# Loading and folding the forward stage's first unit inside the convolution, and squaring into v's far tile

## The chip, the cores and the metric

The kernel runs on one core of one Trainium2 chip. The metric is the device time of one launch in microseconds (us), the median of several runs. Engines are called as in the profile: PE is TensorE (PEld its weight loads), DVE is VectorE, ACT is ScalarE, POOL is GpSimd, SP is SyncE, which here issues most of the DMA transfers; SPq, ACTq and POOLq are the queues of transfers that these engines issue.

## The reference

Two residual layers work on `x`, 16 images of 16 channels of 256 x 256 points in float32. `_gn` is a group norm over 8 groups of two channels.

```python
# layer 0: a circular 3 x 3 convolution, written with Fourier transforms
x = x + _L0_conv_ref(_gn(x), L0_conv_weight)
# layer 1: a Laplace layer
x = x + _L1_conv_ref(_gn(x), ty, tx, weights_pole1, weights_pole2, weights_residue)

# _L1_conv_ref:
alpha = fft2(_gn(x))                                     # per image and channel
A  = 1 / (omega1 - weights_pole1)                        # omega: 2 pi i x frequency
Bm = 1 / (omega2 - weights_pole2)
S  = einsum('ikpq,oikp,xikq->oxik', weights_residue, A, Bm)
output_residue1 = einsum('biox,oxik->bkox', alpha, S)    # mixes channels, per frequency
C  = einsum('biox,oikp->bikpx', alpha, A)
D  = einsum('bikpx,xikq->bikpq', C, Bm)
output_residue2 = einsum('bikpq,ikpq->bkpq', D, weights_residue)
x1 = ifft2(output_residue1).real
E1, E2 = exp(weights_pole1 * ty), exp(weights_pole2 * tx)
F  = einsum('kbpq,bipz->kbiqz', output_residue2, E1)
x2 = einsum('kbiqz,biqx->kizx', F, E2).real              # the transient part
return x1 + x2 / 256 / 256
```

In what follows, v is the result of layer 0, which is the input of layer 1.

## The kernel before

The kernel has four stages, one after the other: the convolution, the forward transform, the mixing of channels, and the inverse transform. Line numbers are those of the kernel before.

**Order and memory.** Each stage opens its own memory pools under a manual schedule: every engine executes its instructions in the order in which the program writes them, and semaphores are set only where two instructions touch the same data. Pools stand as a stack in on-chip memory: a pool that is opened first lies lowest, and a pool that grows moves all that are opened after it. Pools of one stage lie over those of the stage before. In the later stages a tile waits only for the former users of the bytes that it covers (`reuse_waits="tile"`). Where a pool has several buffers, a new tile takes the oldest one and waits for its readers.

**Convolution** (the loop over g, 24 steps for each of 16 images b). A step is 16 small matmuls (L302), which add up in PSUM banks of `ps_conv`; there are six. v is kept as a sum and a difference of the image's two halves, so that each image has four units of a "pair" half, written by the rows r = 0 and 1, and a "far" half, written by r = 2 and 3 three steps later. ScalarE evicts two banks to the tile `pair` when g % 6 is 5 and two to the tile `far` when g % 6 is 2 (L321). Two steps after the far eviction, `mirror` (L267) has DVE add far to pair (L269) and POOL subtract far from pair (L272). ScalarE then squares both results for the statistics (L280): it needs only the sum that `accum_out` gives, and writes the squares themselves to a tile `junk` in a pool of its own. Both squares stand in a list with the step at which they are issued:

```python
squared.append((g + 5, lambda: square(both, 4 + 2 * u, b, bias=shift2[:, b : b + 1])))
squared.append((g + 7, lambda: square(lo, 5 + 2 * u, b)))
```

Four stores to DRAM, one a step (L331, in the list `folded`), take the pair to `vD`. Beside this, SP loads the images for the next steps in 18 parts each (L130, tile `xt`, five buffers); generators compute the statistics of x, the tables of the later stages (`make_coef`, `make_poles`, `make_hat`, `make_c`, mostly on POOL and DVE, with a store of the table `cD` at L643), and the statistics of v for the first 12 images (`v_stats`, L339).

**Forward stage.** It has 64 units (i, b0), channel i and four images from b0 on. For each unit `load_v` (L740) loads 1 MB of `vD` by two transfers to a tile `s` (pool `fold_y`, three buffers, units loaded up to three ahead). `fold` (L746) folds it on DVE (four instructions at L752, L755, L762, L763, L766) and POOL (L762 and L763 for the other half) through a tile `vf` to a tile `vq` (pool `fold_2`, two buffers). `lines` (L770) multiplies for four images j and two halves xo by a table on PE (L774 and L782, into three banks `ps_y`), and ScalarE evicts each bank to the tile `t`, scaled by v's norm (L790). `columns` (L797) does the same for the unit before along the other axis, with the table `fold2` on PE (L817), and DVE writes the spectrum of channel i to the tile `spec` (32 KB a partition, even channels in the pool `spec_even`, odd ones in `spec_odd`, with a pad of 4 KB between). When a channel is complete, `spec` is stored to `aD`; SP issues this store, for the last channel ScalarE does (L973).

The stage begins with the loads of units 0, 1 and 2 (the first on POOL's queue) and the fold of unit 0:

```python
loaded = {u: load_v(*units[u], nc.sync if u else nc.gpsimd) for u in range(3)}
vq = fold(*units[0], loaded.pop(0))
```

In the loop over units the fold of the unit after the next is written ahead of the lines of the present one. In the first two units `rest` is interleaved with the lines: these are v's statistics for the last four images (DVE L349 to L354, PE L357, DVE L359 to L366, PE L374, then a square root).

**Mix stage.** The table `cD` is loaded to the tile `ct` (32 KB a partition, L1005), `first_sums` and `sums` multiply it by weights `w` (PE L1027), DVE and ScalarE spread the result over a tile `sg` (L1047, L1044), spectra of the 16 channels are loaded in groups `abd` (L1102), and PE mixes the channels for each frequency (L1120). The results are stored to `yD`. **The inverse stage** loads them, transforms back along both axes and adds the transients and v.

Of the kernel before, what the change touches and what calls it, by code (L numbers as in the profile page):

```python
# [9 lines left out]
FP = mybir.dt.float32  # L10
AF = mybir.ActivationFunctionType
ALU = mybir.AluOpType
# [4 lines left out]
B = 16  # L17
C = 16
N = 256
P = 128  # L20
# [4 lines left out]
def conv_then_laplace_kernel(ctx: ExitStack, tc: tile.TileContext, a: dict, out: bass.AP):  # L25
# [15 lines left out]
    nc = tc.nc  # L41
    x = a["x"]
# [11 lines left out]
    def const(name, shape, home=cp):  # L54
        t = home.tile(shape, FP, name=name, tag=name)
        later_loads.append((t, a[name]))
        return t
# [10 lines left out]
    vD = []  # L68
    for b in range(B // 4):
        t = dp.tile([P, C, 8 * N + 256], FP, name=f"vD{b}", tag=f"vD{b}")  # L70
# [21 lines left out]
    ptab = ExitStack()  # L92
    tp = ptab.enter_context(tc.tile_pool(name="tables", bufs=1))
    kmask = const("kmask", [P, C], tp)
    fold2 = const("fold2", [P, 2, 64], tp)
    vmr = tp.tile([P, 2, B, C], FP, name="vmr", tag="vmr")


# [12 lines left out]

    p1 = ExitStack()
    wp = p1.enter_context(tc.tile_pool(name="conv_w", bufs=1))
    xp = p1.enter_context(tc.tile_pool(name="xt", bufs=5))
    vp = p1.enter_context(tc.tile_pool(name="v_pair", bufs=3))
    fp = p1.enter_context(tc.tile_pool(name="v_far", bufs=2))
    jp = p1.enter_context(tc.tile_pool(name="junk", bufs=1))
    sp = p1.enter_context(tc.tile_pool(name="stats", bufs=2))  # L120
    sw = p1.enter_context(tc.tile_pool(name="setup", bufs=1))
    pc = p1.enter_context(tc.tile_pool(name="p_conv", bufs=6, space=PSUM))
# [6 lines left out]
    def load_part(t, b, h, i, j):  # L129
        nc.sync.dma_start(  # L130
            out=t[:, i:j].rearrange("p (n r) x -> p n (r x)", r=2),
            in_=x[b][:, 8 * h + i // 2 : 8 * h + j // 2, 0 : 2 * (N + 2)],
        )
# [131 lines left out]
    shift2 = tp.tile([P, B], FP, name="shift2", tag="shift2")  # L265

    def mirror(g, b, u, pair, hi):  # L267
        both, lo = pair[:, :, :, 0], pair[:, :, :, 1]
        nc.vector.scalar_tensor_tensor(  # L269
            both, lo, 1.0, hi, ALU.mult, ALU.add, accum_out=sums[:, b, u : u + 1]  # L270
        )
        nc.gpsimd.tensor_tensor(lo, lo, hi, ALU.subtract)  # L272
        folded.extend((g + 7 + k, b, u, pair, *divmod(k, 2)) for k in range(4))
        squared.append((g + 5, lambda: square(both, 4 + 2 * u, b, bias=shift2[:, b : b + 1])))
        squared.append((g + 7, lambda: square(lo, 5 + 2 * u, b)))

    def square(t, col, b, **by):

        junk = jp.tile([P, 4, N], FP, name="junk", tag="junk")
        nc.scalar.activation(  # L280
            junk,
            t.rearrange("p r j x -> p (r j) x"),
            AF.Square,
            accum_out=sums[:, b, col : col + 1],
            **by,
        )
# [362 lines left out]
    def chain(*gens):  # L649
        for gen in gens:  # L650
            yield from gen

    ready, acc, later, folded, squared, jobs = {}, {}, [], [], [], []
    for j, (_, piece) in enumerate(x_stats(0)):
        if j == 8:
# [26 lines left out]
    early = v_stats(0, B - 4, lambda: pst.tile([P, 512], FP, name="ps_stat", tag="ps_stat"))  # L682
    for g in range(24 * B + 3):
        conv(g)
        past = g - 24 * (B - 4)
        if past in (12, 17, 20, 25, 28, 31):
            next(early, None)
        b, n = divmod(g, 24)
        if b + 2 < B and n % 12 > 2:
            h, k = n // 12, n % 12 - 3  # L690
            if k == 0:
                halves.setdefault(b + 2, []).append(
                    xp.tile([P, 18, N + 2], FP, name="xt", tag="xt")
                )
            load_part(halves[b + 2][h], b + 2, h, PARTS[k], PARTS[k + 1])
        for b, gen in at_step.get(g, ()):
            going.append([b, gen, next(gen)])
        for it in list(going):
            while it[2] is not None and g >= 24 * it[0] - it[2][0]:
                it[2][1]()  # L700
                it[2] = next(it[1], None)
            if it[2] is None:
                going.remove(it)
        run_jobs(g, (psu,) if n in slots and 12 <= past <= 31 else slots.get(n, ()))
        next(tables, None)
# [7 lines left out]
    p1 = ExitStack()  # L713


    def pool(stage, name, bufs=1, **kw):
        return stage.enter_context(tc.tile_pool(name=name, bufs=bufs, reuse_waits="tile", **kw))

    sp = pool(p1, "fold_y", 3)
    f1 = pool(p1, "fold_1")  # L720
    fp = pool(p1, "fold_2", 2)
    lp = pool(p1, "lines", 2)
    a0 = pool(p1, "spec_even")
    kp = pool(p1, "between")
# [3 lines left out]
    bp = pool(p1, "b_const")  # L728
# [6 lines left out]

    kp.tile([P, 1024], FP, name="between", tag="between")
    sgn = bp.tile([P, 2], FP, name="sgn", tag="sgn")
    m, n = cols[:, 16:17], cols[:, 17:18]

    def load_v(i, b0, eng=nc.sync):  # L740
        s = sp.tile([P, 4, 2, N], FP, name="s", tag="s")
        for j in range(0, 4, 2):
            eng.dma_start(out=s[:, j : j + 2], in_=vD[b0 // 4][:, i, j : j + 2])
        return s.rearrange("p b h x -> p h b x")

    def fold(i, b0, s):  # L746


        vf = f1.tile([P, 2, 2, 4, P], FP, name="vf", tag="vf")
        lo, hi = s[:, :, :, 0:P], s[:, :, :, N - 1 : P - 1 : -1]  # L750
        for j in range(4):
            nc.vector.scalar_tensor_tensor(  # L752
                vf[:, 0, 0, j], lo[:, 0, j], vmr[:, 1, b0 + j, i : i + 1], hi[:, 0, j], ALU.add, ALU.add
            )
        nc.vector.tensor_tensor(vf[:, 0, 1], lo[:, 1], hi[:, 1], ALU.add)  # L755


        vq = fp.tile([P, 2, 2, 4, 2, 64], FP, name="vq", tag="vq")

        def again(xo, eng):  # L760
            lo, hi = vf[:, xo, :, :, 0:64], vf[:, xo, :, :, P - 1 : 63 : -1]
            eng.tensor_tensor(vq[:, xo, :, :, 0], lo, hi, ALU.add)  # L762
            eng.tensor_tensor(vq[:, xo, :, :, 1], lo, hi, ALU.subtract)  # L763

        again(0, nc.vector)
        nc.vector.tensor_tensor(vf[:, 1], lo, hi, ALU.subtract)  # L766
        again(1, nc.gpsimd)
        return vq.rearrange("p e o b h x -> p e o b (h x)")

    def lines(i, b0, vf, t, j):  # L770

# [95 lines left out]
    units = [(i, b0) for i in range(C) for b0 in range(0, B, 4)]  # L867
# [64 lines left out]
        )  # L932
        return wt

    loaded = {u: load_v(*units[u], nc.sync if u else nc.gpsimd) for u in range(3)}
    vq = fold(*units[0], loaded.pop(0))
    nc.vector.memset(sgn[:, 0:1], -1.0)
    nc.vector.memset(sgn[:, 1:2], 1.0)
    rest = v_stats(B - 4, B, lambda: pa.tile([P, 512], FP, name="ps_y", tag="ps_y"))
    last, first_weights = None, weights(0)  # L940
    for u in range(len(units) + 1):
        at = units[u] if u < len(units) else None
        if at is not None:
            now = vq
            t = lp.tile([P, 2, 4, 3, P], FP, name="t", tag="t")
            if u + 1 < len(units):
                vq = fold(*units[u + 1], loaded.pop(u + 1))
                if u + 3 < len(units):
                    loaded[u + 3] = load_v(*units[u + 3])
                if u < 2:  # L950
                    next(rest)
            for j in range(2):
                lines(*at, now, t, j)
        if last is not None:
            i, b0 = last[:2]
            if b0 == 0:
                spec = (a0, a1)[i % 2].tile([P, 2, N, B], FP, name="spec", tag="spec")
                psd = pd.tile([P, B, 32], FP, name="psd", tag="psd")
            done = columns(*last, spec, psd)
        if at is not None:  # L960
            for j in range(2, 4):
                lines(*at, now, t, j)
                if u < 2:
                    next(rest, None)
        if u == len(units) - 4:
            first_constants()
        if len(units) - 4 < u < len(units):
            next(first_weights)
        if last is not None:
            first_slots(b0, spec, *done)  # L970
            if b0 == B - 4:
                project(i, psd)
                (nc.sync if i + 1 < C else nc.scalar).dma_start(  # L973
                    out=aD[:, 2 * i : 2 * i + 2], in_=spec.rearrange("p r f b -> p r (f b)")
                )
        last = (*at, t) if at is not None else None
# [11 lines left out]
    tp = pool(p2, "ct")  # L988
# [232 lines left out]
    for g in range(32):  # L1221
# [5 lines left out]
        for n in range(4):  # L1227
# [4 lines left out]
            for m in range(4):  # L1232
                if evict and m < 2:
                    spread(n, (ahead, [z.rearrange("p q n -> p n q") for z in evict]), odds=(m,))
                o, src = mix(4 * n + m, sg, yt)
# [82 lines left out]
    def combine(b0, yk, step=4):  # L1318

        u = up.tile([P, 4, 4, P], FP, name="u", tag="ud")  # L1320
        for j in range(0, 4, step):
            combine_images(yk, slice(b0 + j, b0 + j + step), u[:, j : j + step])
        return u
# [84 lines left out]
    units = [(k, b0) for k in range(C) for b0 in range(0, B, 4)]  # L1408
# [7 lines left out]
    u = combine(0, yk, 1)  # L1416
# [12 lines left out]
    for n, (k, b0) in enumerate(units):  # L1429
# [5 lines left out]
        if b0 % 8 == 0:  # L1435
            both = transient_x(k, b0)
        hs = both[:, b0 % 8 : b0 % 8 + 4]
        begun = [transient(ey_now[:, j], hs[:, j]) if n == 0 else None for j in range(4)]
        if n + 1 < len(units):
# [3 lines left out]
            u = combine(units[n + 1][1], yk)  # L1443
            load_ahead(n + 1)
        r = rp.tile([P, 4, 2, N], FP, name="r", tag="r")
# [172 lines left out]
```

## Time and profile before

| what | value |
|---|---|
| times of three runs | 2611.66, 2622.16, 2623.72 us |
| median | 2622.16 us |
| profiled execution, its own time | 2615.02 us |
| span of its profile | 2613.2 us, 84,265 instructions |
| mean granted PE clock | 0.984 of full |
| busy: PE | 2458.4 us, 94% of the span |
| busy: PEld (beside PE) | 1894.7 us, 73% |
| busy: DVE | 1971.9 us, 75% |
| busy: ACT | 1436.9 us, 55% |
| busy: POOL | 1259.3 us, 48% |
| moved by DMA | 653 MB, 250 GB/s on average |

The profile is of one execution. Its page cuts the span in 40 slices of 65.3 us and gives each engine's busy share in tenths. The row of PE reads `5999999989999999998999999999699999999998`: it starts with 5, is 8 in the 9th and the 19th slice (the convolution's end at 558 us lies in the former, the forward stage's at 1187 us in the latter), and 6 in the 29th, in the inverse stage. Its PE clock row, which is the clock that the throttle granted in tenths, has an 8 in these three slices and 9 elsewhere. In the other views a group of instructions has its line, engine, operation and tiles (written `out<-in`, with partitions x elements), and in brackets the idle time of the engine just before it with what ended that idle time. Most of PE's idle time is in the first slice and at the places just named.

### The profile page before, as it was taken

How to read it: one execution, taken by the hardware profiler on the slowest of the kernel's cores; microseconds unless marked ns; L12 is line 12 of the kernel's file. 1: busy time of each engine (PE TensorE's matmuls, PEld its weight loads, DVE VectorE, ACT ScalarE, POOL GpSimd, SP SyncE). 2: the span in 40 equal slices, each digit the busy share in tenths (PEclk: the TensorE clock that was granted, in tenths of full speed). 3: DMA queues.
4: the chain of work that ended last, by engine and by line, in shares of the span. 5: the costliest groups of instructions: out<-in, count | busy, mean ns of one | idle time of the engine just before them, and what ended most of it. 6: DMA issues, size and time to landing. Idle time of an engine off the chain costs nothing. (4 is left out here: it accounts for less than half of the span.)

```text
span 2613.2 us, 84265 instructions
## 1 busy us (share of the span) xinstructions
PE 2458.4 (94%) x35314; PEld 1894.7 (73%) x35314; DVE 1971.9 (75%) x3772; ACT 1436.9 (55%) x2599; POOL 1259.3 (48%) x1275
## 2 busy tenths in 40 slices
PE   5999999989999999998999999999699999999998
PEld 2454555567777777775888888888588888888887
DVE  7777789748888888887887788787276676667666
ACT  2566666666666666665666666676244444444443
POOL 1333378332333333333656556555555565655553
PEclk9999999989999999998999999999899999999999
DMA  8888888854654654665777787777988888888884
GB/s 273 276 291 286 294 282 302 282 206 167 242 213 191 258 225 192 228 243 175 219 228 227 227 234 229 222 222 225 260 299 286 292 289 283 296 288 294 288 288 173
DMA packets 318010, 653.16 MB, mean 250 GB/s; under 512 B 49174, under 2 KB 163990, under 8 KB 305728
## 3 DMA queue, kind: packets, MB, share of 16 engines
q1 hardware_dynamic: 316464, 640.57, 72.7%
q8 instruction: 278, 4.55, 0.7%
q0 software_dynamic: 896, 3.02, 0.5%
q10 hardware_dynamic: 272, 4.19, 0.4%
q14 instruction: 100, 0.82, 0.1%
HBM read 368.15 MB, written 280.36 MB: 248 GB/s over the span
## 5 line engine op out<-in xcount | busy, mean ns | idle before, releaser
L1330 POOL TENSOR_TENSOR u<-yk 128x512 f32<-128x512 f32 (+1 forms) x268 | 359.4, 1373 | 309.0 <-PE ps_p L1366 243.9
L1120 PE MATMUL ps_mix<-abd,sg 128*64 128x128 f32 x8192 | 471.4, 276 | 34.3 <-DMA yD<-yt 24.0
L1120 PEld LDWEIGHTS ps_mix<-abd,sg 128*64 128x64 f32 x8192 | 452.9, 138 | 64.7 <-issue 54.2
L302 PE MATMUL ps_conv<-xt,wc 32*32 32x512 f32 x12288 | 443.2, 601 | 31.1 <-issue 25.5
L302 PEld LDWEIGHTS ps_conv<-xt,wc 32*32 32x32 f32 x12288 | 251.5, 103 | 209.6 <-issue 127.0
L790 ACT ACTIVATE t<-ps_y,vmr 128x384 f32<-128x384 f32 x512 | 297.0, 580 | 161.8 <-PE ps_y L782 161.8
L1047 DVE STREAM_SHUFFLE sg<-ps_s 128x512 f32<-128x512 f32 (+1 forms) x264 | 328.5, 1319 | 0.0
L774 PE MATMUL ps_y<-tabE,vq 128*128 128x256 f32 x1024 | 313.5, 388 | 11.1 <-DVE vq L763 9.5
L782 PE MATMUL ps_y<-tabO,vq 128*128 128x256 f32 x1024 | 306.3, 381 | 0.0
L1390 PE MATMUL ps_f<-pt,inv 128*128 128x256 f32 x1008 | 300.4, 380 | 0.0
L1391 PE MATMUL ps_f<-hs,ey 128*128 128x256 f32 x1008 | 299.8, 379 | 0.0
L1366 PEld LDWEIGHTS ps_p<-inv,u 128*128 128x128 f32 x2048 | 268.5, 193 | 39.8 <-POOL u L1334 16.0
L272 POOL TENSOR_TENSOR pair<-pair,far 128x1024 f32<-128x1024 f32 x64 | 151.8, 2371 | 299.8 <-DVE pair L269 186.6
L1394 DVE TENSOR_TENSOR r<-ps_f,q 128x256 f32<-128x256 f32 x256 | 107.2, 419 | 247.0 <-ACT q L1393 247.0
L1366 PE MATMUL ps_p<-inv,u 128*128 128x128 f32 x2048 | 276.2, 278 | 14.5 <-POOL u L1334 14.3
L1236 ACT COPY yt<-ps_mix 128x512 f32<-128x512 f32 x352 | 199.7, 583 | 139.0 <-issue 33.5
L774 PEld LDWEIGHTS ps_y<-tabE,vq 128*128 128x128 f32 x1024 | 189.8, 191 | 87.7 <-ACT q L830 51.2
L1393 ACT COPY q<-ps_f 128x256 f32<-128x256 f32 x256 | 95.4, 373 | 275.9 <-PE ps_f L1391 252.4
L1044 ACT ACTIVATE sg<-ps_s,mcol 128x512 f32<-128x512 f32 (+1 forms) x264 | 184.6, 699 | 96.2 <-DVE sg L1047 59.0
L1368 ACT COPY pt<-ps_p 128x512 f32<-128x512 f32 x256 | 151.5, 592 | 137.6 <-PE ps_p L1366 137.6
L762 POOL TENSOR_TENSOR vq<-vf 128x512 f32<-128x512 f32 x64 | 81.3, 1271 | 292.1 <-DVE vf L766 282.0
L782 PEld LDWEIGHTS ps_y<-tabO,vq 128*128 128x128 f32 x1024 | 195.7, 191 | 27.0
(235 smaller groups left out, 3958.4 us busy)
## 6 DMA issues: line engine op xcount, KB each, us to landing
xt<-in_x SPq DMA_DIRECT2D x288, 258.0 KB
vD<-pair SPq DMA_DIRECT2D x256, 256.0 KB
yD<-yt SPq DMA_DIRECT2D x512, 128.0 KB
vl<-vD SPq DMA_DIRECT2D x128, 512.0 KB
out_y<-ol SPq DMA_DIRECT2D x128, 512.0 KB
s<-vD SPq DMA_DIRECT2D x126, 512.0 KB
aD<-spec SPq DMA_DIRECT2D x15, 4096.0 KB
yk<-yD SPq DMA_DIRECT2D x60, 1024.0 KB
```

The lines of the kernel that those rows point to most:

```text
L302: nc.tensor.matmul(acc[r][32 * c : 32 * c + 32], lhsT=ready[b][0][rows, phase, tap], rhs=halves[b][u // 2][rows, q : q + 5 : 4, 2 - tap : ...
L774: nc.tensor.matmul(ps[:, 0:N], lhsT=vf[:, xo, 0, j], rhs=tabE[:, 0 : i + 2 : i + 1], start=True, stop=False, skip_group_check=True,)
L782: nc.tensor.matmul(ps[:, P : P + N], lhsT=vf[:, xo, 1, j], rhs=tabO[:, i : C + 1 : C - i], start=False, stop=True, skip_group_check=True,)
L790: nc.scalar.activation(t[:, xo, j].rearrange("p l n -> p (l n)"), ps[:, 0:384], AF.Copy, scale=vmr[:, 0, b0 + j, i : i + 1],)
L1044: nc.scalar.activation(to[..., k : k + 2], src[odd], AF.Copy, scale=nsgn)
L1047: nc.vector.stream_shuffle(to[..., C + k : C + k + 2], src[1 - odd], swap)
L1120: nc.tensor.matmul(ps[64 * t : 64 * t + 64, j], lhsT=sg[:, f : f + 2].rearrange("p f m -> p (f m)"), rhs=abd[jq][:, :, 2 * t + cc, 2 * jj ...
L1236: (nc.vector.tensor_copy if m >= (2 if late else 3) else nc.scalar.copy)(o, src)
L1330: nc.gpsimd.tensor_tensor(u[:, :, j].rearrange("p b (c n) -> p c b n", c=8), in0, in1, o)
L1366: nc.tensor.matmul(ps[:, at], lhsT=u[:, n], rhs=tab, start=True, stop=True)
L1390: nc.tensor.matmul(ps[:, e], lhsT=tab, rhs=pt[:, e], start=True, stop=False)
L1391: nc.tensor.matmul(ps[:, e], lhsT=ey[:, e], rhs=hs, start=False, stop=True)
```

## The change

Three things are changed.

1. The load of unit 0 moves to step 24 x 15 of the convolution (the first of the last image), and its fold to nine steps later. `first_load` takes for both `s` and `vf` one buffer of the image tiles `xt`, which the last images no longer need; SP issues its two transfers. `fold` is now given its `vf`, and writes units of image group 0 and 2 to `vq0`, a new pool of 8192 bytes a partition that stands under the convolution's pools and is kept through the forward stage, and the others to `fold_2`, which goes from two buffers to one. At the start of the forward stage units 1 and 2 are loaded, unit 1 on POOL's queue and unit 2 on SP's.
2. The pool `junk` is gone. A square writes its unneeded result to the `far` tile of its own unit, which both L269 and L272 read; the first square of a pair is issued one step later than before, so that both stand behind the next far eviction.
3. `fold2` is no longer loaded to the tables' pool with the other constants, but to the pool `b_const` of the forward stage, by a transfer written where that stage starts.

The diff, without empty lines; the body of `fold` that is removed at its old place is the one added at the new, but for `vf` and `vq`:

```diff
     ptab = ExitStack()
     tp = ptab.enter_context(tc.tile_pool(name="tables", bufs=1))
     kmask = const("kmask", [P, C], tp)
-    fold2 = const("fold2", [P, 2, 64], tp)
     vmr = tp.tile([P, 2, B, C], FP, name="vmr", tag="vmr")
...
+    vq0 = ptab.enter_context(tc.tile_pool(name="fold_2_0", bufs=1))
     p1 = ExitStack()
     wp = p1.enter_context(tc.tile_pool(name="conv_w", bufs=1))
     xp = p1.enter_context(tc.tile_pool(name="xt", bufs=5))
     vp = p1.enter_context(tc.tile_pool(name="v_pair", bufs=3))
     fp = p1.enter_context(tc.tile_pool(name="v_far", bufs=2))
-    jp = p1.enter_context(tc.tile_pool(name="junk", bufs=1))
     sp = p1.enter_context(tc.tile_pool(name="stats", bufs=2))
     sw = p1.enter_context(tc.tile_pool(name="setup", bufs=1))
     pc = p1.enter_context(tc.tile_pool(name="p_conv", bufs=6, space=PSUM))
...
         )
         nc.gpsimd.tensor_tensor(lo, lo, hi, ALU.subtract)
         folded.extend((g + 7 + k, b, u, pair, *divmod(k, 2)) for k in range(4))
-        squared.append((g + 5, lambda: square(both, 4 + 2 * u, b, bias=shift2[:, b : b + 1])))
-        squared.append((g + 7, lambda: square(lo, 5 + 2 * u, b)))
-    def square(t, col, b, **by):
-        junk = jp.tile([P, 4, N], FP, name="junk", tag="junk")
+        squared.append((g + 6, lambda: square(hi, both, 4 + 2 * u, b, bias=shift2[:, b : b + 1])))
+        squared.append((g + 7, lambda: square(hi, lo, 5 + 2 * u, b)))
+    def square(junk, t, col, b, **by):
         nc.scalar.activation(
-            junk,
+            junk.rearrange("p r j x -> p (r j) x"),
             t.rearrange("p r j x -> p (r j) x"),
             AF.Square,
             accum_out=sums[:, b, col : col + 1],
...
         for gen in gens:
             yield from gen
+    def fold(i, b0, s, vf):
+        lo, hi = s[:, :, :, 0:P], s[:, :, :, N - 1 : P - 1 : -1]
+        for j in range(4):
+            nc.vector.scalar_tensor_tensor(
+                vf[:, 0, 0, j], lo[:, 0, j], vmr[:, 1, b0 + j, i : i + 1], hi[:, 0, j], ALU.add, ALU.add
+            )
+        nc.vector.tensor_tensor(vf[:, 0, 1], lo[:, 1], hi[:, 1], ALU.add)
+        vq = (vq0 if b0 % 8 == 0 else fp).tile([P, 2, 2, 4, 2, 64], FP, name="vq", tag="vq")
+        def again(xo, eng):
+            lo, hi = vf[:, xo, :, :, 0:64], vf[:, xo, :, :, P - 1 : 63 : -1]
+            eng.tensor_tensor(vq[:, xo, :, :, 0], lo, hi, ALU.add)
+            eng.tensor_tensor(vq[:, xo, :, :, 1], lo, hi, ALU.subtract)
+        again(0, nc.vector)
+        nc.vector.tensor_tensor(vf[:, 1], lo, hi, ALU.subtract)
+        again(1, nc.gpsimd)
+        return vq.rearrange("p e o b h x -> p e o b (h x)")
+    def first_load():
+        t = xp.tile([P, 18, N + 2], FP, name="xt", tag="xt").rearrange("p r x -> p (r x)")
+        s = t[:, 0 : 8 * N].rearrange("p (b h x) -> p b h x", b=4, h=2)
+        for j in range(0, 4, 2):
+            nc.sync.dma_start(out=s[:, j : j + 2], in_=vD[0][:, 0, j : j + 2])
+        vf = t[:, 8 * N : 16 * N].rearrange("p (e h b x) -> p e h b x", e=2, h=2, b=4)
+        return s.rearrange("p b h x -> p h b x"), vf
     ready, acc, later, folded, squared, jobs = {}, {}, [], [], [], []
     for j, (_, piece) in enumerate(x_stats(0)):
         if j == 8:
...
     early = v_stats(0, B - 4, lambda: pst.tile([P, 512], FP, name="ps_stat", tag="ps_stat"))
     for g in range(24 * B + 3):
         conv(g)
+        if g == 24 * (B - 1):
+            first_unit = first_load()
+        if g == 24 * (B - 1) + 9:
+            vq = fold(0, 0, *first_unit)
         past = g - 24 * (B - 4)
         if past in (12, 17, 20, 25, 28, 31):
             next(early, None)
...
     sp = pool(p1, "fold_y", 3)
     f1 = pool(p1, "fold_1")
-    fp = pool(p1, "fold_2", 2)
+    fp = pool(p1, "fold_2")
     lp = pool(p1, "lines", 2)
     a0 = pool(p1, "spec_even")
     kp = pool(p1, "between")
...
     kp.tile([P, 1024], FP, name="between", tag="between")
     sgn = bp.tile([P, 2], FP, name="sgn", tag="sgn")
+    fold2 = bp.tile([P, 2, 64], FP, name="fold2", tag="fold2")
+    nc.sync.dma_start(out=fold2, in_=a["fold2"])
     m, n = cols[:, 16:17], cols[:, 17:18]
     def load_v(i, b0, eng=nc.sync):
...
         for j in range(0, 4, 2):
             eng.dma_start(out=s[:, j : j + 2], in_=vD[b0 // 4][:, i, j : j + 2])
         return s.rearrange("p b h x -> p h b x")
-    def fold(i, b0, s):
...
-        return vq.rearrange("p e o b h x -> p e o b (h x)")
     def lines(i, b0, vf, t, j):
...
         )
         return wt
-    loaded = {u: load_v(*units[u], nc.sync if u else nc.gpsimd) for u in range(3)}
-    vq = fold(*units[0], loaded.pop(0))
+    loaded = {u: load_v(*units[u], nc.sync if u > 1 else nc.gpsimd) for u in range(1, 3)}
     nc.vector.memset(sgn[:, 0:1], -1.0)
     nc.vector.memset(sgn[:, 1:2], 1.0)
     rest = v_stats(B - 4, B, lambda: pa.tile([P, 512], FP, name="ps_y", tag="ps_y"))
...
             now = vq
             t = lp.tile([P, 2, 4, 3, P], FP, name="t", tag="t")
             if u + 1 < len(units):
-                vq = fold(*units[u + 1], loaded.pop(u + 1))
+                vf = f1.tile([P, 2, 2, 4, P], FP, name="vf", tag="vf")
+                vq = fold(*units[u + 1], loaded.pop(u + 1), vf)
                 if u + 3 < len(units):
                     loaded[u + 3] = load_v(*units[u + 3])
                 if u < 2:
```

## The prediction

> **What bounds the kernel now.** TensorE is busy 94% of the page's span, so time is lost where its row dips: the start, the 9th slice (the seam between convolution and forward stage) and the 19th (the seam between forward stage and mix). I read the timeline at the first seam, the two parts the change touches, and then the second. Columns are start, duration, engine, line, op, tiles, count, and in brackets the idle time before and its releaser.
>
> ```profile
> 519.56 38.50 PE L302 MATMUL ps_conv<-xt,wc 32*32 32x512 f32 x1134
> ...
> 557.28 1.38 POOL L743 DMA_DIRECT2D s<-vD  x2
> ...
> 560.75 2.34 POOL L272 TENSOR_TENSOR pair<-pair,far 128x1024 f32<-128x1024 f32 x1 [2.09 <-DVE pair L269]
> ...
> 563.08 0.61 DVE L752 SCALAR_TENSOR_TENSOR vf<-s,vmr 128x128 f32<-128x128 f32 x2 [2.42 <-DMA s<-vD]
> ...
> 564.90 0.61 DVE L752 SCALAR_TENSOR_TENSOR vf<-s,vmr 128x128 f32<-128x128 f32 x2 [1.21 <-DMA s<-vD]
> ...
> 567.36 1.22 DVE L766 TENSOR_TENSOR vf<-s 128x1024 f32<-128x1024 f32 x1
> ...
> 567.59 1.19 PE L774 MATMUL ps_y<-tabE,vq 128*128 128x256 f32 x2 [9.53 <-DVE vq L763]
> ...
> 571.19 1.22 PE L774 MATMUL ps_y<-tabE,vq 128*128 128x256 f32 x2 [1.56 <-POOL vq L763]
> ...
> 575.49 1.26 DVE L351 TENSOR_SCALAR vs<-vs 128x4 f32<-128x4 f32 x1
> ...
> 578.15 0.28 PE L357 MATMUL ps_y<-vs,g 128*128 128x4 f32 x2
> ...
> 580.33 0.60 PE L774 MATMUL ps_y<-tabE,vq 128*128 128x256 f32 x2
> ```
>
> TensorE's convolution ends at 558.06. It waits for the first unit's load (issued 557.28), then for its fold (563.08 to 567.45), once more for POOL's half of it (571.15), and begins unit 1 at 580.33: 22.3 us for eight "lines" (an L774 and an L782) that take 0.86 us each at full clock (581.19 to 582.05), 6.9 in all. So at most 15.4 us lie here.
>
> The second seam, same view, at the end of the forward stage:
>
> ```profile
> 1167.06 0.32 SPq L1005 DMA_DIRECT2D ct<-cD  x1
> ...
> 1189.48 2.50 PE L1027 MATMUL ps_s<-ct,w 64*32 64x256 f32 x64 [2.35 <-ACT w L924]
> ...
> 1191.31 0.38 ACTq L973 DMA_DIRECT2D aD<-spec  x1
> ...
> 1196.71 0.72 DVE L1047 STREAM_SHUFFLE sg<-ps_s 128x256 f32<-128x256 f32 x1
> ```
> ```profile
> 1203.09 2.58 SPq L1102 DMA_DIRECT2D abd<-aD  x4
> ...
> 1216.36 7.21 PE L1120 MATMUL ps_mix<-abd,sg 128*64 128x128 f32 x128
> ```
>
> Here ct (4.19 MB) is loaded behind the last forward unit, 22 us before L1027 uses it. The last store of a spec leaves at 1191.31 and is complete when SP goes on, at 1203.09: 11.8 us for 4.19 MB. L1027, L1047 and L1044 build the first sg, and mixing starts at 1216.36.
>
> **What the Trainium skill says.** "TensorE: Matmul & The Clock Gate", Part 1: after an idle window of about 3.4 us TensorE's clock is halved until about as long a busy one. The trace agrees: mean granted clock 0.57 in 558 to 568 and 0.68 in 568 to 581; the first lines are 1.7 us apart. "SBUF — State Buffer", "SBUF: two separate sides": VectorE and GpSimd lock a port pair for a whole instruction. It agrees: L351 on 128x4 takes 1.26 us and ends with POOL's L762. "DMA: Bandwidth & Descriptors", "Anatomy of one DMA": about 2 us plus bytes over 436 GB/s, an estimate of 11.6 us for ct; the trace's 11.8 for an equal store is used.
>
> **Part 1: load and fold of unit 0 in the last image.** The two loads (SP) and the fold move ahead; unit 1's load takes unit 0's place on POOL's queue, unit 2's and the first half of unit 3's take SP's. In the instruction order the fold stands on DVE behind the mirror (L269) that ran at 534.99: 1.14+3x0.69+1.22 = 4.4 us in an idle gap of 4.8; POOL's half is 2x1.27 us, and POOL is busy 10.7 of 26 us there. SP issues the loads near 534, behind stores; 1 MB lands near 540. Then the next mirror slips by up to 2.5 us, POOL's L272 by up to 4, and ScalarE's eviction by 2, which the third pair of accumulator banks covers but for about 0.2. Cost 0 to 1.
>
> The seam then runs so. Lines 1 to 3 go at 558.1 to 560.7 into three ps_y banks. ScalarE's written order is far, square, t, square, t, square, t, square, then t's: with 1.2 us a square and 0.6 a t, and the third square held to 563.1 (it now overwrites far, which L272 reads), the three t end at 561.2, 563.0 and 565.0. Lines 4 to 6 follow these and end at 565.9. Next on TensorE is L357, the last images' statistics. Its input stands on DVE behind fold(1), whose loads arrive like unit 0's did: L766 ends at 568.6, L351 is held by POOL's L762 to 569.9. So L357 runs at 570.0. **This wait takes the place of the removed one.** Lines 7 and 8 take 1.7 us (full clock) or 3.4 (halved), L374 needs L366 near 572.8, and unit 1 begins at 573.1 to 574.0, its first line perhaps still slow (0.7). POOL's half of unit 1 is ready at 571.2. Gain 580.33 less that: 5.6 to 7.2. I take 6.0; with the loads 2 us later or sooner, 4 to 8. From there each unit is bound by TensorE (100 busy in 600 to 700), so it lasts.
>
> **Part 2: junk into far.** 128 squares keep their cost. Their far may be reused only by ScalarE itself. The first of each two moves behind the far eviction: 1.26+1.2+1.2 = 3.7 us in a half period of 3.1 to 3.3. Going through the 64 units of the trace, the next pair eviction slips by 0.5 us in most and by at most 1.5; the bank is needed 3 steps of 1.09 us after its last matmul, of which eviction takes 1.3. So nearly free; where setup evictions fall in the same slot 0.2 to 0.5 us may show. I take 1, bounds 0 to 5.
>
> **Part 3: memory.** fold2 leaves the tables (512 B a partition), vq0 adds 8192 under the forward pools, fold_2 loses 8192. So all pools above fold_2 lie 512 B lower, while the mix stage's do not move. ct covers bytes 144,608 to 177,376. The spec of odd channels began at 177,760; now at 177,248. **They overlap by 128 bytes.** In the changed program ct's load waits for the last aD store (issued by ScalarE) and for the copies into that spec; before, it did not. Its queue, SP, holds abd01's loads behind it; these waited for that store anyway. TensorE's L1027 waits for ct, and all of the first sg for L1027.
>
> All times less 6.0: store issued 1185.3, complete 1197.1; ct lands 11.8 later, 1208.9. L1027's first group takes 1.25 at the idle clock, so L1047 begins at 1210.2 instead of 1196.71. From L1047 to mixing took 19.65: mixing at 1229.8 against 1216.36. DVE's and POOL's other work of this stretch is done by then, and abd01's 1 MB goes behind ct on the same engines. Delay at this seam 19.5, bounds 17 (the shuffles, freed of other work, faster) and 24 (abd01's loads share the bandwidth, 1 MB at 430 GB/s is 2.4, and slow clock). Mixing is bound by TensorE (19.84 busy of 20 us in 1220 to 1240), so nothing gives it back.
>
> fold2's own load moves to SP late in the convolution with p2k, kgrp and mcol, behind a wait for a cD store: up to 3 us for x loads used some 10 us later. Nothing, up to 1.
>
> **Sum.** -6.0+1+19.5 = +14.5 us. The profiled execution took 2615.02 (span 2613.2), 7.1 below the median 2622.16; the four times lie in two pairs, so I add to their mean, 2618.1: 2632.6. Against no change, 0.5% is 13 us, about what a measurement of this kernel can tell.
>
> **Rivals.** (a) Not slower: ct's wait is covered. If mixing at 1216.36 was in truth set by abd01's loads, or the first sg could start without ct, only part 1 is left: -6+1, 2613. For it: abd01 also waits for that store. Against: abd01 was issued by 1205.7 and DMA moved only 5 GB/s from 1209 to 1214, so it had landed; L1027 used ct at 1189.48, the ct wait is in the program. It decides as soon as ct lands before about 1195. 10%.
> (b) The squares hold ScalarE up in the convolution: if 30 of 64 units lose 0.2 to 0.3 us, 8 more, 2640. For: TensorE already waited 7.1 us for L321. Against: slack of 1.7 us. 8%.
> (c) The fold isn't early or its wait stays: the order shows it four mirrors before the end, so only L357's wait can grow; gain 2 instead of 6, 2636. 6%.
> (d) More of the first seam is won (L357 early, clock kept): gain 10, 2628. 6%.
>
> **Numbers.** Forecast 70%, its delta 9 to 20. Slower by over 0.5% is three quarters of it, (b), (c) and a little of (d): 0.70. Within: the rest of the forecast, half of (a): 0.21. Faster: 0.09, (a) with a slow base. Range: base 2612 to 2622 and delta 6 to 23, leaving out most of (a): 2617 to 2645.
>
> **What shows it.** Right: TensorE's L774 starts within 1 us of the convolution's end; a wait of 3 to 5 us at L357; unit 1 near 574; ct's load issued near 1197, not 1167; L1027 idle some 20 us on DMA ct; mixing near 1230. Wrong: ct issued before 1185; idle time at L302 grown by over 5 us; mixing's start before 1220.

## The result and the profile after

The changed kernel takes 2634.35 us (median of six runs, 2627.21 to 2637.96); the kernel before took 2615.92 us (six runs, 2610.73 to 2623.72). The ratio is 1.0061, with a 95% interval of 1.0041 to 1.0082: slower by 10.7 to 21.5 us, about 16. The profiled execution took 2632.37 us, its span 2630.4 us, 17.2 more than the span before.

The page's row of PE, busy tenths in 40 slices, and the clock row under it show where. First the changed kernel:

```profile
PE   5899999999999999995999999999699999999998
...
PEclk9999999999999999997999999999799999999999
```

The 9th slice, with the first seam, rose from 8 to 9; the 19th, with the second, fell from 8 to 5, and its clock from 8 to 7. So something was won at the first seam and more lost at the second. (The second slice, inside the convolution, fell from 9 to 8; how much that stage varies without any edit is shown below.)

**The first seam**, in the timeline of the changed kernel. L300 is L302 of before, L786 is L774, L349 and L355 are L351 and L357; L656 is the fold's first line, L268 and L271 are the mirror's two:

```profile
524.54 36.40 PE L300 MATMUL ps_conv<-xt,wc 32*32 32x512 f32 x1068
...
531.70 0.99 SPq L679 DMA_DIRECT2D xt<-vD  x2
...
539.12 3.26 DVE L656 SCALAR_TENSOR_TENSOR xt<-xt,vmr 128x128 f32<-128x128 f32 x4
...
545.36 1.22 DVE L268 SCALAR_TENSOR_TENSOR pair<-pair,far 128x1024 f32<-128x1024 f32 x1
...
548.91 2.38 POOL L271 TENSOR_TENSOR pair<-pair,far 128x1024 f32<-128x1024 f32 x1
...
560.88 0.70 PE L786 MATMUL ps_y<-tabE,vq 128*128 128x256 f32 x2
...
567.84 0.70 PE L786 MATMUL ps_y<-tabE,vq 128*128 128x256 f32 x2 [1.25 <-ACT t L802]
...
571.32 1.25 DVE L349 TENSOR_SCALAR vs<-vs 128x4 f32<-128x4 f32 x1
...
572.72 0.56 PE L355 MATMUL ps_y<-vs,g 128*128 128x4 f32 x2 [3.74 <-DVE vs L349]
573.13 1.20 PE L786 MATMUL ps_y<-tabE,vq 128*128 128x256 f32 x2
...
577.12 0.75 PE L786 MATMUL ps_y<-tabE,vq 128*128 128x256 f32 x2
```

The two loads are issued at 531.70, the fold stands on DVE at 539.12, and the first line follows the last convolution matmul at once (560.88 against 560.94). Then TensorE waits for the evictions of `t`, and 3.74 us for the statistics. Unit 1 begins at 577.12, 16.2 us after the convolution's end; before it was 22.3 (580.33 less 558.06). But the convolution ended 2.9 us later, so unit 1 begins only 3.2 us earlier.

**The second seam**, same view of the changed kernel:

```profile
1188.25 0.39 ACTq L985 DMA_DIRECT2D aD<-spec  x1
...
1199.65 0.32 SPq L1017 DMA_DIRECT2D ct<-cD  x1
1200.15 2.64 SPq L1114 DMA_DIRECT2D abd<-aD  x4
...
1212.09 4.99 PE L1039 MATMUL ps_s<-ct,w 64*32 64x256 f32 x96 [28.02 <-DMA ct<-cD]
...
1214.18 0.74 DVE L1059 STREAM_SHUFFLE sg<-ps_s 128x256 f32<-128x256 f32 x1
...
1232.23 7.21 PE L1132 MATMUL ps_mix<-abd,sg 128*64 128x128 f32 x128
```

The load of ct is issued 11.4 us after the last store of a spectrum, where before it was issued 24 us ahead of it. The first sums wait 28.02 us for it instead of 2.35 for other data, and mixing starts 43.98 us after the store's issue; before, 25.05 (1216.36 less 1191.31). That is 18.9 us. The 17.2 us are then made up of -6.1 at the first seam, 18.9 at the second, 2.9 in the convolution, 0.15 in the forward stage between (611.13 us from unit 1 to the store, against 610.98) and 1.3 after the start of mixing (1398.2 us to the end of the span, against 1396.8).

### The profile page after: what moved, and what is told of

It reads as the page before. It is cut to its first block, busy times and chain, and to the rows that moved or that the text cites. A ratio compares the mean times of both kernels' runs of the same rounds, so it can differ in the third digit from the quotient of the medians.

```text
span 2630.4 us, 84205 instructions
## 1 busy us (share of the span) xinstructions
PE 2464.6 (94%) x35314; PEld 1894.7 (72%) x35314; DVE 1980.9 (75%) x3772; ACT 1438.3 (55%) x2599; POOL 1254.0 (48%) x1275
## 4 chain that ended last, share of the span: by engine, by line
PE 68%; DVE 13%; DMA 9%; SPq 4%; issue 3%; ACT 2%; POOL 1%; DVEq 0%; ACTq 0%; POOLq 0%
PE ps_conv L300 10%; PE ps_y L786 9%; PE ps_y L794 8%; PE ps_mix L1132 8%; PE ps_p L1378 7%; PE ps_f L1402 7%; PE ps_f L1403 7%; PE ps_x L829 5%; DMA yD<-yt 4%; DVE sg L1059 3%; PE ps_s L1039 2%; DMA xt<-in_x 2%; PE ps_h L1362 2%; SPq L1146 1%; PE psd L814 1%
## 5 line engine op out<-in xcount | busy, mean ns | idle before, releaser
L1342 POOL TENSOR_TENSOR u<-yk 128x512 f32<-128x512 f32 (+1 forms) x268 | 351.4, 1344 | 316.7 <-PE ps_p L1378 243.9
L300 PE MATMUL ps_conv<-xt,wc 32*32 32x512 f32 x12288 | 447.8, 602 | 28.7 <-issue 22.3
L300 PEld LDWEIGHTS ps_conv<-xt,wc 32*32 32x32 f32 x12288 | 250.0, 103 | 213.2 <-issue 115.9
L1059 DVE STREAM_SHUFFLE sg<-ps_s 128x512 f32<-128x512 f32 (+1 forms) x264 | 328.7, 1320 | 0.0
L786 PE MATMUL ps_y<-tabE,vq 128*128 128x256 f32 x1024 | 312.9, 387 | 1.8 <-ACT t L802 1.8
L271 POOL TENSOR_TENSOR pair<-pair,far 128x1024 f32<-128x1024 f32 x64 | 151.7, 2371 | 293.7 <-DVE pair L268 151.6
L1378 PE MATMUL ps_p<-inv,u 128*128 128x128 f32 x2048 | 276.1, 278 | 12.9 <-POOL u L1346 12.8
L786 PEld LDWEIGHTS ps_y<-tabE,vq 128*128 128x128 f32 x1024 | 189.3, 190 | 78.6 <-ACT q L842 50.3
L666 POOL TENSOR_TENSOR vq<-vf 128x512 f32<-128x512 f32 x63 | 80.2, 1273 | 287.2 <-DVE vf L670 276.1
L794 PEld LDWEIGHTS ps_y<-tabO,vq 128*128 128x128 f32 x1024 | 195.1, 191 | 26.7
```

Of the source, the lines that this page charges most:

```text
L300: nc.tensor.matmul(acc[r][32 * c : 32 * c + 32], lhsT=ready[b][0][rows, phase, tap], rhs=halves[b][u // 2][rows, q : q + 5 : 4, 2 - tap : ...
L786: nc.tensor.matmul(ps[:, 0:N], lhsT=vf[:, xo, 0, j], rhs=tabE[:, 0 : i + 2 : i + 1], start=True, stop=False, skip_group_check=True,)
L794: nc.tensor.matmul(ps[:, P : P + N], lhsT=vf[:, xo, 1, j], rhs=tabO[:, i : C + 1 : C - i], start=False, stop=True, skip_group_check=True,)
L1059: nc.vector.stream_shuffle(to[..., C + k : C + k + 2], src[1 - odd], swap)
L1342: nc.gpsimd.tensor_tensor(u[:, :, j].rearrange("p b (c n) -> p c b n", c=8), in0, in1, o)
L1378: nc.tensor.matmul(ps[:, at], lhsT=u[:, n], rhs=tab, start=True, stop=True)
```

## The experiments

All six were timed against the kernel before; e1 to e4 on one chip, where that one took 2617.43 us (30 runs), e5 and e8 on another, where it took 2625.23 us (37 runs). The expectations give times for a base near 2616, so those of e5 and e8 are compared by their ratios. Two lengths are read from every trace, since they don't depend on what came earlier: the first seam, from the last convolution matmul to unit 1's first line, and the second, from the issue of the last store to the first mixing matmul.

| kernel | convolution's end | first seam | second seam | ratio to before, 95% |
|---|---|---|---|---|
| before | 558.06 | 22.27 | 25.05 | |
| after | 560.94 | 16.18 | 43.98 | 1.0061 (1.0041 to 1.0082) |
| e1, pad of 128 bytes | 563.22 | 15.91 | 24.08 | 0.9982 (0.9968 to 0.9995) |
| e2, before with overlap | 564.46 | 21.53 | 43.06 | 1.0059 (1.0042 to 1.0076) |
| e3, before with new squares | 563.15 | 21.35 | 22.47 | 0.9993 (0.9979 to 1.0006) |
| e4, e1 with later statistics | 565.55 | 12.01 | 23.76 | 0.9949 (0.9930 to 0.9968) |
| e5, e1 with old squares | 567.34 | 15.02 | 22.48 | 0.9990 (0.9977 to 1.0003) |
| e8, after with ct in three loads | 560.81 | 16.24 | 40.94 | 1.0051 (1.0036 to 1.0066) |

### e1: the overlap taken away

```diff
-    kp.tile([P, 1024], FP, name="between", tag="between")
+    kp.tile([P, 1024 + 32], FP, name="between", tag="between")
```

> The changed kernel with the pad `between` larger by 128 bytes a partition, so that the spectrum of odd channels begins where ct ends. Theory (ct waits for the last store of a spectrum only because of 128 shared bytes): ct's load is issued some 20 us before the forward stage ends, near 1165 to 1177, TensorE's first sums (L1039) start within 3 us of the stage's last L829 group, mixing starts near 1213 instead of 1232; the time is 19 us less than the changed kernel's and 2 to 4 less than the kernel before. Rival 1 (the load is late for another reason of the new program, such as the order on SP's queue or the single fold_2 buffer): nothing moves, 2634, ct issued near 1200. Rival 2 (with ct early the loads of abd become the bound): 5 to 10 us less than the changed kernel only, mixing near 1223.

Measured: 2613.56 us, ratio 0.9982 (0.9968 to 0.9995). The timeline of this kernel at the second seam:

```profile
1166.35 0.32 SPq L1017 DMA_DIRECT2D ct<-cD  x1
...
1188.79 1.96 PE L1039 MATMUL ps_s<-ct,w 64*32 64x256 f32 x64 [2.35 <-ACT w L936]
...
1190.61 0.39 ACTq L985 DMA_DIRECT2D aD<-spec  x1
...
1214.69 7.21 PE L1132 MATMUL ps_mix<-abd,sg 128*64 128x128 f32 x128
```

With 32 more floats in a pad that nothing reads, ct's load is issued 24 us ahead of the store again, the sums wait 2.35 us for other data, and the second seam is back to 24.08. Both rivals fall. The rest of the change, without its overlap, is faster than before by 4.7 us (1.3 to 8.4); 2 to 4 were expected.

### e2: the overlap alone

```diff
-    kp.tile([P, 1024], FP, name="between", tag="between")
+    kp.tile([P, 1024 - 128], FP, name="between", tag="between")
```

> The kernel before with the pad `between` smaller by 512 bytes a partition and nothing else: ct and the spectrum of odd channels share 128 bytes as in the changed kernel. Theory: this alone costs what the second seam lost, mixing starts 19 to 20 us later than in the kernel before (near 1235 to 1236), the time is near 2635. The convolution and the first seam stay (convolution's end near 558, unit 1 near 580). Rival (the loss needs the other edits): 2616, mixing near 1216.

Measured: 2635.27 us, ratio 1.0059 (1.0042 to 1.0076), 11 to 20 us more. The timeline of this kernel at both seams:

```profile
554.40 10.06 PE L302 MATMUL ps_conv<-xt,wc 32*32 32x512 f32 x256
...
585.99 0.60 PE L774 MATMUL ps_y<-tabE,vq 128*128 128x256 f32 x2
...
1196.97 0.38 ACTq L973 DMA_DIRECT2D aD<-spec  x1
...
1208.36 0.32 SPq L1005 DMA_DIRECT2D ct<-cD  x1
...
1220.81 6.79 PE L1027 MATMUL ps_s<-ct,w 64*32 64x256 f32 x128 [28.02 <-DMA ct<-cD]
...
1240.03 7.21 PE L1120 MATMUL ps_mix<-abd,sg 128*64 128x128 f32 x128
```

A program with none of the change's steps, only a pad that is 512 bytes smaller, shows the same picture: ct issued 11.4 us behind the store, 28.02 us of wait, a second seam of 43.06. So the overlap is enough, and e1 shows that nothing else of the change does it. One expectation was wrong: the convolution didn't end near 558. It ended at 564.46 (554.40 + 10.06), with its instructions those of before, and all later times stand later by about as much. That matters for the squares, in e3 and e5.

### e3: the squares alone

```diff
-        squared.append((g + 5, lambda: square(both, 4 + 2 * u, b, bias=shift2[:, b : b + 1])))
-        squared.append((g + 7, lambda: square(lo, 5 + 2 * u, b)))
+        squared.append((g + 6, lambda: square(hi, both, 4 + 2 * u, b, bias=shift2[:, b : b + 1])))
+        squared.append((g + 7, lambda: square(hi, lo, 5 + 2 * u, b)))
+    jp.tile([P, 4, N], FP, name="junk", tag="junk")
...
-        junk = jp.tile([P, 4, N], FP, name="junk", tag="junk")
```

> The kernel before with the squares' part alone: both squares write to far, the first a step later; the junk pool is kept, unused, so that no address moves. The changed kernel's convolution ended 2.9 us later than before (560.94 against 558.06). Theory A (the squares behind the far eviction, and far held longer, push the evictions): the convolution ends 2 to 4 us later here too, time 2617 to 2620. Theory B (the 2.9 come from the loads and the fold put into the convolution, from moved constants' loads, or from the spread between executions): the convolution ends within 1 us of the kernel before, time 2616.

Measured: 2616.25 us, ratio 0.9993 (0.9979 to 1.0006): between 5.5 us faster and 1.6 slower. The convolution ended at 563.15, five later than in the trace before, which taken alone would speak for theory A. But e2 ended it 1.3 later still with the old squares, and this kernel isn't slower over its 14 runs. The end of one execution's convolution varies by more than the effect in question. The total speaks for theory B. The waits view, for TensorE's waits for evictions between 60 and 570 us (us in total, times, longest), of the kernel before, of e2 (both with the old squares), of e3 and of e1 (both with the new ones):

```profile
PE ps_conv L302 <- ACT pair L321: 1.4, 3, 0.6
```
```profile
PE ps_conv L302 <- ACT pair L321: 4.3, 2, 2.7
```
```profile
PE ps_conv L303 <- ACT pair L322: 1.3, 2, 1.0
PE ps_conv L303 <- ACT far L322: 0.6, 1, 0.6
```
```profile
PE ps_conv L300 <- ACT pair L319: 8.0, 5, 3.1
PE ps_conv L300 <- ACT far L278: 0.6, 1, 0.6
```

With the old squares 1.4 and 4.3 us, with the new ones 1.9 and 8.6 (and 2.4, 2.9 and 1.8 in after, e4 and e8). By themselves these sums don't decide. One step further back, what the large ones wait for is not a square. The eviction behind the longest of e1's waits, and that wait (two lines of the timeline, of two engines):

```profile
148.27 1.27 ACT L319 ACTIVATE pair<-ps_conv,xq 128x512 f32<-128x512 f32 x2 [3.86 <-DMA vD<-pair]
...
149.01 4.03 PE L300 MATMUL ps_conv<-xt,wc 32*32 32x512 f32 x54 [3.08 <-ACT pair L319]
```

ScalarE itself waited here, 3.86 us, for a store of v out of a `pair` tile. That is so for 7.8 of e1's 8.0 us, and for the 2.7 us of e2, with the old squares.

### e4: the statistics out of the first seam's way

On top of e1:

```diff
-                if u < 2:
+                if u == 0:
                     next(rest)
             for j in range(2):
                 lines(*at, now, t, j)
+            if u == 1:
+                next(rest), next(rest)
...
                 lines(*at, now, t, j)
-                if u < 2:
-                    next(rest, None)
+            if u == 0:
+                next(rest), next(rest)
+            if u == 1:
+                next(rest, None)
```

> The changed kernel with the pad larger by 128 bytes, and the statistics of the last four images issued later among the first units' lines: L355 stands behind all eight lines of unit 0 instead of six, L372 behind four lines of unit 1 instead of ahead of them. Theory (the two matmuls of the statistics hold TensorE at the first seam, since their input stands behind the fold of unit 1): unit 1 begins 12 to 13 us after the convolution's end instead of 16.2, and the time is 3 to 4 us less than with the pad alone. Rival (POOL's half of unit 1's fold, which ended 12.8 us after the convolution in the changed kernel, or the three ps_y banks, take the wait's place): less than 1 us gained.

Measured: 2608.36 us, ratio 0.9949 (0.9930 to 0.9968). The timeline of this kernel at the first seam:

```profile
554.39 11.16 PE L300 MATMUL ps_conv<-xt,wc 32*32 32x512 f32 x297
...
565.48 0.70 PE L786 MATMUL ps_y<-tabE,vq 128*128 128x256 f32 x2
...
575.33 0.59 PE L794 MATMUL ps_y<-tabO,vq 128*128 128x256 f32 x2
577.35 0.36 PE L355 MATMUL ps_y<-vs,g 128*128 128x4 f32 x2 [1.42 <-DVE vs L349]
577.56 0.68 PE L786 MATMUL ps_y<-tabE,vq 128*128 128x256 f32 x2
...
579.03 0.67 PE L786 MATMUL ps_y<-tabE,vq 128*128 128x256 f32 x2 [0.36 <-DVE vs L357]
```

Lines 7 and 8 of unit 0 now run while the statistics are still on DVE, the wait at L355 falls to 1.42 us (3.49 in e1, 3.74 in the changed kernel), and the seam from 15.91 to 12.01. So it was L355 that held TensorE there, as the prediction had it. Not all of the 3.9 us is waiting: after 1.42 us of idle time the next lines run at 0.59 to 0.68 us for each two matmuls, after the 3.74 us of the changed kernel at 1.06 to 1.20. The granted clock of the changed kernel shows why (a stretch, its length, PE busy with its instructions, the clock, then DMA):

```profile
568.90:570.50 1.60, 0.07 (x1) 1.00 1.04 415
570.70:572.70 2.00, 0.00 (x0) 0.50 1.02 389
572.70:577.30 4.60, 4.58 (x13) 0.50 0.57 187
577.50:580.00 2.50, 2.50 (x13) 1.00 1.00 397
```

The Trainium skill, "TensorE: Matmul & The Clock Gate", Part 1: The HAM clock gate, says that an idle window of about 3.4 us halves the clock. That idle time halves it is so here, but less was enough: the clock fell 1.6 us into the wait, in e8 1.0 us into one of 4.26 us, and in e5 a wait of 2.59 us in all was followed by lines at 1.06 to 1.20 us as well. In e4 the clock stayed at 1.00.

This version beats both kernels: 13 us less than the kernel before by the ratio (8.4 to 18.3), 9.1 by the medians. Against e1 that is 8.6 us by the ratios and 5.2 by the medians, where 3 to 4 were expected; the seam accounts for 3.9, and what the rest is, if it is more than the spread of six runs, these runs don't show.

### e5: the old squares beside the rest of the change

On top of e1, for the first 15 images, the old steps and a junk tile of their own:

```diff
-        squared.append((g + 6, lambda: square(hi, both, 4 + 2 * u, b, bias=shift2[:, b : b + 1])))
-        squared.append((g + 7, lambda: square(hi, lo, 5 + 2 * u, b)))
+        own_junk = jq if b + 1 < B else hi.rearrange("p r j x -> p (r j) x")
+        squared.append((g + 5 + b // (B - 1), lambda: square(own_junk, both, 4 + 2 * u, b, bias=shift2[:, b : b + 1])))
+        squared.append((g + 7, lambda: square(own_junk, lo, 5 + 2 * u, b)))
+    jq = vq0.tile([P, 2, 2, 4, 2, 64], FP, name="vq", tag="vq")
...
```

> The changed kernel with the pad larger by 128 bytes, and for the first 15 images the squares as before: the first at step g + 5, both into a junk tile, which lies in vq0's still unused bytes. If the squares' part costs what was predicted (0 to 1 us), the time is that of the pad alone within the spread (2610 to 2616) and TensorE's waits for L319's evictions of pair do not shrink by more than 1 us. If far, held longer, costs some 3 us: 2 to 4 us less than with the pad alone, and a convolution that ends near 558. The kernels so far ended it at 558.1, 560.9, 563.2, 564.5, 563.2 and 565.5, the 564.5 with the convolution of before unchanged, so the end of one execution alone decides nothing.

Measured: 2622.78 us on the second chip, ratio 0.9990 (0.9977 to 1.0003), against e1's 0.9982 (0.9968 to 0.9995): the old squares show no gain, though the two intervals leave room for one of some 3 us. TensorE's waits for evictions of pair came to 2.6 us, 5.4 less than in e1 and so outside the 1 us expected; but e1's were waits for stores of v, as e3 showed. And this kernel has a delay of its own making, in the last image behind the fold (three lines of the timeline, of three engines):

```profile
546.92 0.69 DVE L670 TENSOR_TENSOR vq<-xt 128x512 f32<-128x512 f32 x1 [2.24 <-ACT vq L282]
...
556.21 1.15 ACT L282 ACTIVATE far<-pair,shift 128x1024 f32<-128x1024 f32 x1 [4.02 <-POOL pair L271]
...
559.26 8.08 PE L304 MATMUL ps_conv<-xt,wc 32*32 32x512 f32 x140 [2.38 <-ACT pair L323]
```

The junk tile lies in vq0's bytes, so the fold's first write to vq waits 2.24 us for the last square that used them as junk. POOL's half of the fold and the mirrors behind it slip with it, a square waits 4.02 us for POOL's mirror (1.23 in e1), the next eviction of pair comes late, and TensorE waits 2.38 us for it. From the first matmul of the last image to the convolution's end 31.5 us pass here, in the seven other traces 26.7 to 27.2. So some 4.5 us of this execution (an estimate, 31.5 less 27.0) are not the old squares', and e5 decides less than e3.

### e8: ct in three loads

```diff
-    nc.sync.dma_start(out=ct, in_=cD)
+    nc.sync.dma_start(out=ct[:, 0:3], in_=cD[:, 0:3])
+    nc.sync.dma_start(out=ct[:, 3, 0:4], in_=cD[:, 3, 0:4])
+    nc.sync.dma_start(out=ct[:, 3, 4:8], in_=cD[:, 3, 4:8])
```

> The changed kernel, overlap kept, with ct's load split in three transfers, of which only the last (0.5 MB, ct's last 4096 bytes a partition) touches the 128 shared bytes; the sums need it only from the third of their first four groups on. Theory 1 (the wait belongs to the tile: any write to ct waits for every former user of any of its bytes): all three go after the last store, 2632 to 2637, mixing near 1232. Theory 2 (the wait belongs to the bytes a transfer writes): two transfers go near 1165, the last near 1199 and lands some 3 us later, the sums' first two groups run near 1187, the third waits to about 1203, and mixing starts some 5 us later than with the pad: near 2619.

Measured: 2639.18 us on the second chip, ratio 1.0051 (1.0036 to 1.0066). The timeline of this kernel at the second seam:

```profile
1199.43 0.32 SPq L1017 DMA_DIRECT2D ct<-cD  x1
1199.80 0.43 SPq L1018 DMA_DIRECT2D ct<-cD  x1
1200.27 0.43 SPq L1019 DMA_DIRECT2D ct<-cD  x1
...
1209.35 6.30 PE L1041 MATMUL ps_s<-ct,w 64*32 64x256 f32 x96 [25.50 <-DMA ct<-cD]
...
1228.96 7.21 PE L1134 MATMUL ps_mix<-abd,sg 128*64 128x128 f32 x128
```

All three wait for the store, though the first two touch none of the shared bytes: in this program the wait belongs to the tile. Theory 1 holds for the wait. What it left out is that the first sums need only the first two transfers: they start 9.9 us after the first issue instead of 12.4, and the second seam is 3 us shorter (40.94). Here cutting the transfer doesn't get round the wait. What does is a tile that doesn't touch the bytes (e1); two tiles in its place were not tried.

## Why the prediction was right, point by point

**The second seam** was read from addresses, and its path holds step by step. Store to ct's issue: 11.8 us predicted, 11.4 measured. Landing: 11.8 predicted; the sums start 12.4 after the issue. First group to L1059: 1.25 predicted, 2.1 measured. From there to mixing: 19.65 predicted, 18.05 measured; the lower bound had allowed for faster shuffles (that they were freed of other work is argued, not shown). Sum from store to mixing 44.5 predicted, 43.98 measured; the loss 19.5 predicted, 18.9 measured. That the sum is so close is in part luck: single steps were off by up to 1.6 us, in both directions. Averaged over all traces it is 19.9 (43.5 in the two with the whole ct behind the store, 23.6 in the five without overlap). Rival (a), that the wait is covered, falls with the 28.02 us and with e2.

**The first seam** too. The prediction's times hold from the convolution's end: lines 4 to 6 end 8.0 us after it (7.8 predicted), DVE's fold of unit 1 ends 10.3 after it (10.5), L349 11.6 (11.8), L355 runs at 11.8 (11.9). Lines 7 and 8 took 3.8 us at the halved clock (573.13 to 576.90), where the prediction had 3.4, or 1.7 at the full one, and unit 1's first line began 16.2 after the end, just past the predicted 15.0 to 15.9. Gain 6.1 against 6.0; averaged over before, e2 and e3 on one side (21.7) and after, e1, e5 and e8 on the other (15.8), 5.9. That L355's wait takes the place of the removed one is shown by e4. So rival (c), a gain of 2, is out, and so is rival (d), a gain of 10 with L355 early: e4 had to move L355 to get there (22.3 less 12.0).

**The squares and the convolution.** 1 us was taken, with bounds 0 to 5. The trace after showed 2.9 in the convolution, which looks like rival (b) at a third of its size. But e2, with the convolution of before, ended it at 564.46, and e3 put the squares' cost between -5.5 and 1.6 us. So the 2.9 can't be charged to the change: the trace of before happened to have the earliest end of eight, 558.06 to 567.34. The difference is made early. From the convolution's first matmul to the first of the 14th image, before and e2, with the same instructions, took 441.7 and 448.7 us, and the six others, e3 among them, lie between these two (442.7 to 447.0). Whether the cost is 0 or 1 these runs can't say. Two of the prediction's figures here are misread: the 7.1 us for L321 are waits of the weight loads (PEld), the matmuls waited 1.4; and three steps of 1.09 us less 1.3 leave a slack of 2.0 us, not 1.7.

**The fold in the last image** was mis-sized in one term: its four L656 were taken at 1.14 us in all and took 3.26, so that DVE's part ran 6.3 us (539.12 to 545.45) instead of 4.4. In the idle order of before they had taken 0.61 for two; here POOL's L271 (539.28 to 541.70) began just behind the first of them. The prediction had named this conflict of DVE and POOL and used it for L351 at the seam, but not for the fold, which it had put directly behind a mirror, where POOL begins. POOL's L271 of the next mirror did slip, to 548.91. It cost TensorE nothing: the last image took 26.7 to 27.0 us in the three traces without the fold and 26.7 to 27.2 in four with it; the fifth is e5, with its own delay.

**The sum.** -6.0 + 1 + 19.5 = 14.5 was predicted; the two seams give 12.8, and the times 16 (10.7 to 21.5), or 18.4 between the medians. The base mattered as much: the prediction took 2618.1 between the median 2622.16 of three runs and the profiled 2615.02; six runs gave 2615.92. That 2632.6 came within 2 us of the measured 2634.35 is therefore in part luck, since a base 2.2 us too high made up for a difference that was 1.5 to 3.9 too small. (The base and difference that the prediction gives for its range make 2618 to 2645, not 2617.)

## What to carry to other kernels

When a change moves a pool, compare the addresses of the next stage's first tiles with the last tiles of the stage before, not only the pools that the diff names: 128 shared bytes turned a load that was hidden into 19 us of TensorE's time, and 128 bytes of padding gave them back. When a wait is removed at a seam, look for the next instruction on the same queue whose input is late; here statistics of four images, two small matmuls, held back lines that were ready. And where single executions of one program differ by several us in a stage, measure lengths from an event inside the trace, and take the effect of an edit from many runs. An experiment that borrows bytes, as e5 does, brings waits of its own; look for them in its trace before reading its total.

## What had not been expected of the hardware

- The end of the convolution lay between 558.06 and 567.34 us in eight traces; in the two whose convolution has the very instructions of before, at 558.06 and 564.46. What sets it apart from one execution to the next is not settled here.
- Some DVE operations aren't merely slower beside one of GpSimd's, they end when that one does. Of the fold's four L656, the one that met POOL's L271 took 2.47 us, to 0.15 us behind the end of L271, and the three others 0.34 each. L349 and L350 on 128x4 took 1.25 and 1.18 us beside POOL's L666 and L667 and ended within 0.03 us of them; L351 and L352 of that size took 0.16 us directly after. Not every operation does this: in e1 three of L189, statistics of x, took 1.88 us in all beside an L271 of 2.38. The prediction had the wait for L349, but not for the fold.
- TensorE's clock was halved after waits well under 3.4 us, but not after each of them. Between 60 and 600 us of the eight traces, each of the 12 idle times of more than 3 us had a halving in it or within 3.4 us of its end, and so had 11 of the 25 of 2 to 3 us.
